# Turning a block's sums by VectorE squares and DRAM in the fourth layer of a graph network

## The chip, the cores and the metric

The kernel runs on one core of a Trainium2 chip. The metric is the device time of one execution in microseconds. A core has five engines that each work through their own instructions in order: TensorE (PE; its weight loads are shown as PEld), VectorE (DVE), ScalarE (ACT), GpSimd (POOL) and SyncE (SP), which here only starts DMAs. They wait for one another through semaphores.

## What is computed

Four layers over 4096 nodes with 256 features each share one adjacency matrix. The change concerns the fourth:

```python
def _cos_normalize(x):
    n = jnp.linalg.norm(x, axis=-1, keepdims=True)
    return x / jnp.maximum(n, COS_EPS)
Qn = _cos_normalize(features @ Wq.T)
Kn = _cos_normalize(features @ Wk.T)
raw_att = Kn @ Qn.T
att = jnp.where(adj > 0, raw_att, NEG) * TEMP
att = jax.nn.softmax(att, axis=1)
prop_fea = att @ features
...
return (1.0 - KEEP_RATIO) * prop_fea + KEEP_RATIO * features
# around it
x = _layernorm(x + _L3_gnn_ref(x, adj, L3_gnn_Wq, L3_gnn_Wk), axis=-1)
```

KEEP_RATIO is 0.5, so a row of the result is 1.5 times the row of x plus half the weighted mean of the features, normalised. The kernel uses that each centred row of x has a known sum, so that the sum of a turned row stands for the softmax's denominator.

## The kernel before

All arrays are float32 on the chip. The fourth layer (cosine_attention, from L1099) takes the 4096 result rows in NB = 8 blocks of 512. For each block it goes over NT = 32 units j of 128 neighbours. A unit's scores are one product of 128x128 by 128x512 (L1115), written to a bank of PSUM: pz holds two (named p), used for even units, ps holds two (named g), used for odd ones after the first block. ScalarE takes the exponential (L1119), VectorE multiplies a pair of units by the mask (L1127) and forms sums and differences of the weights (mix_weights, L434 to L436). TensorE then adds seven products of 128x128 by 128x256 per pair into four accumulating banks, acc 0 to 3 (product, L444), a scheme with seven products in place of eight. A product is two records in the trace.

The text puts the products LAG = 4 units behind the scores: at step i it writes the scores of unit i and then half the products of the pair of unit i - 4. After the last products of a block comes outputs(b). There first_half (L449 to L453) and second_half (L457, L458) combine the four accumulators into c, the "quarters": the features lie on the 128 partitions, the block's 512 rows along the free side. The output wants it the other way round. So turned (L1139) transposes c by TensorE, 128x128 at a time, eight times a block, into the g banks, four to a bank. The row sums of a bank give the inverse of the denominator (halves_of_inverse, L1145 to L1147), rest (L1160 to L1164) adds the scaled row to y, which holds 1.5 x (L1247), and takes its statistics, normalise (L184 and the lines of the root before it) scales the rows, and store (L1167) sends 512 rows of y to the output on SP's queue. The buffers y are two. The last block has an ending of its own.

The order on each engine in this layer is not written by hand, but for the ending. A planner sets it when the program is built: it follows the text's order where it can, and takes an instruction from further on in the text where it expects an engine to be free and the operands to be there. In the three layers before, the order of TensorE, VectorE and ScalarE is the text's.

The masks come by GpSimd's queue (L1046), 512 KB for four units, into four buffers. SP's queue has nothing but the output stores once the first block of this layer is past its first part.

The kernel already turns other data by VectorE and DRAM: turning_apart (L127 to L135) transposes squares of 32x32, stores them with one DMA, and fetches them with four.

Of the kernel before, what the change touches and what calls it, by code (L numbers as in the profile page):

```python
# [9 lines left out]
FP = mybir.dt.float32  # L10
# [4 lines left out]
OP = mybir.AluOpType  # L15
AX = mybir.AxisListType
PSUM = bass.MemoryType.PSUM

P = 128
D = 256  # L20
KC = D // P
QB = 4
QW = QB * P
# [5 lines left out]
def kernel(  # L29
# [27 lines left out]
    nc = tc.nc  # L57
# [4 lines left out]
    def pool(stack, name, bufs, **kw):  # L62
        return stack.enter_context(tc.tile_pool(name=name, bufs=bufs, reuse_waits="tile", **kw))
# [3 lines left out]
    fin = ctx.enter_context(tc.tile_pool(name="fin", bufs=2))  # L67
    fin1 = ctx.enter_context(tc.tile_pool(name="fin1", bufs=1))
# [83 lines left out]
    def one_row(mv, k, y):  # L152
        st = fin.tile([P, 6], FP, name="bn")
        nc.vector.bn_stats(st, y)
        nc.vector.bn_aggr(mv[:, k, :], st)
# [7 lines left out]
    def end_root(v, r, n, eng=nc.vector):  # L163

        s = fin.tile([P, n], FP, name=f"s{n}")
        eng.tensor_tensor(s, r, r, OP.mult)
        eng.tensor_tensor(s, s, v, OP.mult)
        eng.tensor_scalar(s, s, -0.5, 1.5, OP.mult, OP.add)
        eng.tensor_tensor(r, r, s, OP.mult)
# [7 lines left out]
    def begin_root(mv):  # L177
        n = mv.shape[1]
        v = fin.tile([P, n], FP, name=f"v{n}")
        nc.vector.tensor_scalar_add(v, mv[:, :, 1], EPS)  # L180
        return v, first_root(v, n), n

    def scale_row(y, mv, r, k):
        nc.vector.tensor_scalar(y, y, mv[:, k, 0:1], r[:, k:k + 1], OP.subtract, OP.mult)  # L184

    def lift_mean(mv, v, r, eng=nc.vector):

        eng.tensor_tensor(v, v, r, OP.mult)
        eng.tensor_tensor(mv[:, :, 0], mv[:, :, 0], v, OP.subtract)

    def normalise(ys, mv, lift=False):
        v, r, n = begin_root(mv)
        end_root(v, r, n)
        if lift:
            lift_mean(mv, v, r)
        for k, y in enumerate(ys):
            scale_row(y, mv, r, k)
# [249 lines left out]
    def first_half(c, one, acc):  # L447

        nc.scalar.copy(one, acc[3][:, :HW])  # L449
        nc.vector.tensor_tensor(c[:, :2, :], one.unsqueeze(1).to_broadcast([P, 2, HW]),  # L450
                                acc[0].rearrange("p (h i) -> p h i", h=2), OP.add)
        nc.vector.tensor_tensor(c[:, 2, :], c[:, 1, :], acc[1][:, :HW], OP.add)
        nc.vector.tensor_tensor(c[:, 3, :], c[:, 2, :], acc[1][:, HW:], OP.add)  # L453

    def second_half(c, acc):

        nc.vector.tensor_tensor(c[:, 1:3, :], c[:, 1:3, :], acc[2][:, :HW].unsqueeze(1).to_broadcast([P, 2, HW]), OP.add)  # L457
        nc.vector.tensor_tensor(c[:, 1, :], c[:, 1, :], acc[2][:, HW:], OP.add)  # L458

    def quarters(c, k):  # L460

        lo = k % 2 * P
        return [c[:, q, lo:lo + P] for q in ((0, 3), (1, 2))[k // 2]]
# [623 lines left out]
    def cosine_attention(co, tail):  # L1087
# [4 lines left out]
        with ExitStack() as lay:  # L1092
# [1 line left out]
            sb = pool(lay, "co_sb", LAST + 1)  # L1094
            yp = pool(lay, "co_y", 2)
            cp = pool(lay, "co_parts", 1)
            co.turning = (pool(lay, "co_turn", 1), None,
                          pool(lay, "co_turn_far", 2, space=bass.MemoryType.DRAM))

            pa = pool(lay, "co_pa", 1, space=PSUM)  # L1100
            pz = pool(lay, "co_pz", 2, space=PSUM)
            ps = pool(lay, "co_ps", 2, space=PSUM)
            ov = out.rearrange("(t p) d -> p t d", p=P)
            mixed, acc, prob, mix, y = {}, {}, {}, {}, {}
            twice = cp.tile([P, 1], FP, name="twice")
            nc.gpsimd.memset(twice, 2.0 / D)

            def bank():
                return ps.tile([P, QW], FP, name="g")

            def scores(b, j):
                if (b, j // MJ) not in co.mask:
                    co.load_mask(b, j // MJ)
                p = bank() if b and j % 2 else pz.tile([P, QW], FP, name="p")
                nc.tensor.matmul(p.rearrange("p (k i) -> p k i", k=QB), T[j // QB][:, 0, j % QB], T[b][:, 1],  # L1115
                                 start=True, stop=True)
                if j % 2 == 0:
                    prob[b, j // 2] = sb.tile([P, 2, QW], FP, name="prob")
                nc.scalar.activation(prob[b, j // 2][:, j % 2, :], p, AF.Exp)  # L1119
# [11 lines left out]
            def one_product(b, g, n):  # L1131
                product(acc[b], prob[b, g], mix[b, g], mixed[g // 2][:, g % 2], g, n)

            def turned(c, h):

                po = bank().rearrange("p (k f) -> p k f", f=D)
                for k in range(2):
                    for n, quarter in enumerate(quarters(c, 2 * h + k)):
                        nc.tensor.transpose(po[:, k, n * P:(n + 1) * P], quarter, ident)  # L1139
                return po  # L1140

            def halves_of_inverse(po):

                rden = fin.tile([P, 2], FP, name="rden2")
                nc.vector.tensor_reduce(rden, po, AX.X, OP.add)  # L1145
                nc.vector.tensor_scalar_mul(rden, rden, 2.0 / D)
                nc.vector.reciprocal(rden, rden)  # L1147
                return rden

            def sums_turned(b, c, h):  # L1150

                sums = acc[b][3][:, HW + 2 * h:HW + 2 * h + 2]
                for k in range(2):
                    for n, quarter in enumerate(quarters(c, 2 * h + k)):
                        nc.tensor.matmul(sums[:, k:k + 1], quarter, twice, start=(h == k == n == 0), stop=(n == 1),  # L1155
                                         skip_group_check=True)
                return sums

            def rest(b, k, po, rden, mv):
                nc.vector.scalar_tensor_tensor(y[b][:, k, :], po[:, k % 2, :], rden[:, k % 2:k % 2 + 1], y[b][:, k, :],  # L1160
                                               OP.mult, OP.add)
                st = fin.tile([P, 6], FP, name="bn")
                nc.vector.bn_stats(st, y[b][:, k, :])  # L1163
                nc.vector.bn_aggr(mv, st)  # L1164

            def store(b, k, n, eng):
                eng.dma_start(ov[:, b * QB + k:b * QB + k + n, :], y[b][:, k:k + n, :])  # L1167

            def outputs(b):
                c = cp.tile([P, 4, HW], FP, name="quarters")  # L1170
                first_half(c, cp.tile([P, HW], FP, name="one"), acc[b])
                second_half(c, acc[b])
                mv = fin.tile([P, QB, 2], FP, name="mv")
                for h in range(2):
                    po = turned(c, h)
                    rden = halves_of_inverse(po)
                    for k in (2 * h, 2 * h + 1):
                        rest(b, k, po, rden, mv[:, k, :])
                normalise([y[b][:, k, :] for k in range(QB)], mv)
                store(b, 0, QB, nc.sync)  # L1180

            def ending(b):

# [46 lines left out]
            for i in range(len(units) + LAG):  # L1230
                if i < len(units):
                    b, j = units[i]
                    scores(b, j)
                    if j % 2:
                        weights(b, j // 2)
                    if (b, j) == (0, 3):
                        tail(bank, cp)
                    if (b, j) in steps:
                        n, step = steps[b, j]
                        co.prepare(bank, n, step, X[:, n * QB:(n + 1) * QB, :])  # L1240
                if i >= LAG:
                    b, j = units[i - LAG]
                    if j == 0:
                        acc[b] = [pa.tile([P, QW], FP, name=f"acc{n}") for n in range(4)]
                    if j == NT - 8:
                        y[b] = yp.tile([P, QB, D], FP, name="y")
                        nc.scalar.mul(y[b], X[:, b * QB:(b + 1) * QB, :D], 1.5)  # L1247
                    if i - LAG < len(units) - 2 * LAST:
                        for n in range(7)[:4] if j % 2 == 0 else range(7)[4:]:
                            one_product(b, j // 2, n)  # L1250
                        if j == NT - 1:
                            outputs(b)
            with tc.manual_schedule(engines={mybir.EngineType.DVE, mybir.EngineType.Activation}):
                ending(NB - 1)

# [25 lines left out]
    with ExitStack() as weights1, ExitStack() as den1, ExitStack() as weights3:  # L1281
# [26 lines left out]
        co = Cosine(weights3)  # L1308
# [36 lines left out]
```

## Time and profile before

| | |
|---|---|
| runs | 2817.45, 2818.91, 2821.47 us; median 2818.91 |
| the profiled execution | 2817.77 us, of which the span from the first to the last instruction is 2816.0 us |
| granted clock of TensorE | 0.997 |
| the fourth layer's blocks | borders about 76.84 us apart, 2270.5 to 2731.6 us; the end at 2816 |
| TensorE's transposes L1139 | 64 in all, 273 ns each as the records show them |
| VectorE's transposes of 128x512, L127 | about 0.70 us each |
| mask loads of the layer, L1046 | one each 9.5 us, 5.7 us to landing |

The time in the table is that of whole executions. The profile is of one execution. Its page gives for each engine the busy time and its share of the span; a matmul's busy time reaches into that of the next one, so the distance from start to start is its price where TensorE doesn't idle. In lists by time, "x3" is three such instructions merged, and brackets hold the idle time before and what ended it.

### The profile page before, as it was taken

The page shows a single profiled execution, that of the slowest core. Times are in us where ns is not written, and L with a number is a line of the kernel's source. Part 1 is how long each engine was busy: PE and PEld are TensorE (multiplying, and loading weights), DVE is VectorE, ACT ScalarE, POOL GpSimd, SP SyncE. Part 2 cuts the span into 40 slices and gives each one's busy share as a digit, 9 for nine tenths or more (in the row PEclk, how much of TensorE's full clock was granted, in tenths as well). Part 3 has the DMA queues.
Part 4 walks back from the last instruction along what each step waited for, and adds up shares of the span by engine and source line. Part 5 has one row for each costly group of instructions (what it writes and reads, how often), then busy time and mean ns, then how long its engine had stood idle before and what let it go on. Part 6 is the DMA issues. An engine that isn't in the chain of part 4 may idle for free. (4 is left out here: it accounts for less than half of the span.)

```text
span 2816.0 us, 50179 instructions
## 1 busy us (share of the span) xinstructions
PE 2784.7 (99%) x19505; PEld 1434.6 (51%) x19505; DVE 2274.4 (81%) x3034; ACT 1695.6 (60%) x2641; POOL 1050.6 (37%) x983
## 2 busy tenths in 40 slices
PE   9999999999999999999999999999999999999998
PEld 5333333333443333333333334788887777777776
DVE  8899999999677788887887888888877766666665
ACT  8899999999246666666666665555565422222222
POOL 0001001001039878879778782454455100000000
PEclk9999999999999999999999999999999999999999
DMA  7566766665439899898998997576767544444441
GB/s 208 109 136 137 141 144 139 132 136 105 90 96 191 186 184 194 189 194 179 193 186 186 193 184 182 169 201 179 201 186 235 94 67 60 61 67 61 60 58 32
DMA packets 243650, 404.59 MB, mean 144 GB/s; under 512 B 25185, under 2 KB 126033, under 8 KB 242514
## 3 DMA queue, kind: packets, MB, share of 16 engines
q0 software_dynamic: 104176, 182.74, 41.0%
q1 hardware_dynamic: 132720, 211.41, 25.2%
q10 hardware_dynamic: 6514, 7.23, 0.7%
q8 instruction: 153, 2.51, 0.4%
q14 instruction: 87, 0.71, 0.1%
HBM read 332.27 MB, written 35.73 MB: 131 GB/s over the span
## 5 line engine op out<-in xcount | busy, mean ns | idle before, releaser
L830 DVE TENSOR_TENSOR prob<-p,mask 128x1024 f32<-128x1024 f32 x512 | 619.8, 1221 | 168.2 <-ACT p L820 162.1
L820 ACT ACTIVATE p<-p,shift 128x1024 f32<-128x1024 f32 x512 | 555.6, 1088 | 317.8 <-PE p L818 317.8
L310 PE MATMUL acc<-prob,V 128*32 128x512 f32 x6144 | 664.0, 592 | 1.2 <-DVE prob L300 1.2
L297 ACT ACTIVATE prob<-row,dst 128x512 f32<-128x512 f32 x1020 | 635.1, 712 | 0.6
L300 DVE SCALAR_TENSOR_TENSOR prob<-prob,mask 128x2048 f32<-128x2048 f32 x256 | 580.1, 2284 | 25.9 <-ACT prob L297 25.2
L840 POOL TENSOR_TENSOR den<-den,prob 128x1024 f32<-128x1024 f32 x220 | 558.1, 2537 | 95.8 <-DVE prob L830 84.9
L818 PE MATMUL p<-qT,kT 64*64 64x512 f32 x4096 | 531.1, 590 | 0.8 <-DVE prob L830 0.8
L854 PE MATMUL acc<-prob,V 64*64 64x512 f32 x4096 | 529.9, 589 | 0.0
L310 PEld LDWEIGHTS acc<-prob,V 128*32 128x32 f32 x6144 | 197.3, 110 | 453.0 <-issue 431.6
L444 PE MATMUL acc<-mix,mixed 128*128 128x256 f32 x1440 | 390.0, 380 | 1.7 <-DVE quarters L458 1.0
L854 PEld LDWEIGHTS acc<-prob,V 64*64 64x64 f32 x4096 | 157.4, 133 | 282.1 <-issue 280.3
L818 PEld LDWEIGHTS p<-qT,kT 64*64 64x64 f32 x4096 | 154.4, 133 | 277.4 <-issue 257.4
L444 PEld LDWEIGHTS acc<-mix,mixed 128*128 128x128 f32 x1440 | 272.2, 190 | 42.1 <-PE acc L444 2.9
L1127 DVE TENSOR_TENSOR prob<-prob,mask 128x1024 f32<-128x1024 f32 x128 | 156.4, 1222 | 168.9 <-ACT prob L1119 167.0
L90 POOL COPY tick<-prob 128x1 f32<-128x1 f32 x35 | 38.5, 1100 | 642.4 <-DVE prob L300 641.5
L444 PE MATMUL acc<-prob,X 128*128 128x256 f32 x960 | 250.5, 380 | 8.6 <-DVE quarters L450 8.6
L846 POOL DMA_DIRECT2D den<-prob x240 | 226.8, 945 | 59.0 <-DVE prob L830 26.0
L1046 POOL DMA_DIRECT2D mask<-in_adjT x64 | 47.7, 745 | 516.7 <-DVE prob L1127 430.3
L565 DVE SCALAR_TENSOR_TENSOR prob<-r,own,mask 128x512 f32<-128x512 f32 x252 | 177.1, 743 | 64.0 <-POOL mix L436 21.3
L444 PEld LDWEIGHTS acc<-prob,X 128*128 128x128 f32 x960 | 181.6, 190 | 92.2 <-issue 62.4
L1119 ACT ACTIVATE prob<-p 128x512 f32<-128x512 f32 x144 | 86.1, 598 | 222.1 <-PE p L1115 209.8
L1119 ACT ACTIVATE prob<-g 128x512 f32<-128x512 f32 x112 | 66.8, 596 | 194.0 <-PE g L1115 194.0
(220 smaller groups left out, 2810.3 us busy)
## 6 DMA issues: line engine op xcount, KB each, us to landing
mask<-in_adjT SPq DMA_DIRECT2D x254, 512.0 KB
den<-prob POOLq DMA_DIRECT2D x240, 512.0 KB, 5.2
mask<-edges SPq DMA_DIRECT2D x512, 64.0 KB
mask<-in_adjT POOLq DMA_DIRECT2D x64, 512.0 KB, 5.7
edges<-in_adj POOLq DMA_DIRECT2D x32, 512.0 KB, 10.0
far<-squares SPq DMA_DIRECT2D x16, 512.0 KB
den<-prob SPq DMA_DIRECT2D x16, 512.0 KB
row<-far SPq DMA_DIRECT2D x7, 1024.0 KB
```

Source lines behind the costliest of these rows:

```text
L297: nc.scalar.activation(z[:, h, :], r, AF.Relu, bias=-1.0, scale=dst[:, j, h:h + 1])
L300: nc.vector.scalar_tensor_tensor(z, z, 1.0, mask[m][:, j % MJ, :].unsqueeze(1).to_broadcast([P, H, QW]), OP.add, OP.mult)
L310: nc.tensor.matmul(acc[b][h * G:(h + 1) * G, n, :], part, prob[b, j][:, h, :], start=(j == 0), stop=(j == NT - 1))
L444: nc.tensor.matmul(acc[at][:, half * HW:(half + 1) * HW], w, a, start=(g == 0 and half == 0), stop=(g == NP - 1), skip_group_check=True)
L565: nc.vector.scalar_tensor_tensor(z[:, n, :], r, ga.own[:, j:j + 1], mask[:, n, :], OP.add, OP.mult)
L818: nc.tensor.matmul(p[c * d:(c + 1) * d, r, :], kT[half, c, at:at + d], qT[half, c, cols], start=True, stop=True)
L820: nc.scalar.activation(p, p, AF.Exp, bias=shift)
L830: nc.vector.tensor_tensor(z, p, mask[m][:, j % MJ, :].unsqueeze(1).to_broadcast([P, KC, QW]), OP.mult)
L840: nc.gpsimd.tensor_tensor(to, to, flat, OP.add)
L846: nc.gpsimd.dma_start(to, flat, accum_op=OP.add)
L854: nc.tensor.matmul(acc[b][c][r * d:(r + 1) * d, :], V[half, j, r * d:(r + 1) * d], prob[b, j][half, r, :], start=(j == 0), stop=(j == NH - 1))
L1127: nc.vector.tensor_tensor(z, z, co.mask[b, 2 * g // MJ][:, lo:lo + 2, :], OP.mult)
```

## The change

For all blocks but the last the sums are no longer transposed by TensorE. outputs(b) now makes c and calls squares_far for each half. That turns two quarters of 128x256 by VectorE in squares of 32x32 into sq, starts four stores on SP's queue, each of 32 partitions and in pieces of 32 numbers (128 B), to the DRAM tile away, and one load of 128 rows of 2 KB from it to the tile t. What was done with the turned sums is in outputs_far(b), which the text calls in the next block after the products of unit 10: the sums of t's rows, the inverse, the addition to y, the statistics, the normalisation and the store. The tiles sq, and t of the second half, lie in buffers of the pool fin1 that earlier layers use; t of the first half is new.

```diff
             def outputs(b):
                 c = cp.tile([P, 4, HW], FP, name="quarters")
                 first_half(c, cp.tile([P, HW], FP, name="one"), acc[b])
+                squares_far(b, 0, (c[:, 0, :], c[:, 3, :]))
                 second_half(c, acc[b])
-                mv = fin.tile([P, QB, 2], FP, name="mv")
-                for h in range(2):
-                    po = turned(c, h)
-                    rden = halves_of_inverse(po)
-                    for k in (2 * h, 2 * h + 1):
-                        rest(b, k, po, rden, mv[:, k, :])
-                normalise([y[b][:, k, :] for k in range(QB)], mv)
-                store(b, 0, QB, nc.sync)
+                squares_far(b, 1, (c[:, 1, :], c[:, 2, :]))
...
+            def squares_far(b, h, both):
+
+                B = P // QB
+                sq = fin1.tile([P, QW], FP, name=f"kept{h}").rearrange("p (a k c s) -> p a k c s", a=QB, k=2, c=KC)
+                for n, quarter in enumerate(both):
+                    nc.vector.transpose(sq[:, :, :, n, :].rearrange("p a k s -> p k a s"),
+                                        quarter.rearrange("p (k a r) -> p k a r", k=2, r=B))
+                away = far.tile([B, QB, QW // P, QB, B], FP, name="away")
+                for q in range(QB):
+                    nc.sync.dma_start(away[:, :, :, q, :].rearrange("r a m s -> r (a m) s"),
+                                      sq[q * B:(q + 1) * B].rearrange("r a k c s -> r (a k c) s"))
+                t = (fin1 if h else cp).tile([P, QW], FP, name="kept2")
+                nc.sync.dma_start(t, away.rearrange("r a m q s -> a r (m q s)"))
+                back[b, h] = t.rearrange("p (k f) -> p k f", k=2)
+
+            def outputs_far(b):
+                mv = fin.tile([P, QB, 2], FP, name="mv")
+                rden = fin.tile([P, QB], FP, name="rden4")
+                for h in range(2):
+                    nc.vector.tensor_reduce(rden[:, 2 * h:2 * h + 2], back[b, h], AX.X, OP.add)
+                nc.vector.tensor_scalar_mul(rden, rden, 2.0 / D)
+                nc.vector.reciprocal(rden, rden)
+                for k in range(QB):
+                    nc.vector.scalar_tensor_tensor(y[b][:, k, :], back[b, k // 2][:, k % 2, :], rden[:, k:k + 1], y[b][:, k, :],
+                                                   OP.mult, OP.add)
+                    one_row(mv, k, y[b][:, k, :])
+                normalise([y[b][:, k, :] for k in range(QB)], mv)
+                store(b, 0, QB, nc.sync)
...
                         if j == NT - 1:
                             outputs(b)
+                    if b and j == 10:
+                        outputs_far(b - 1)
```

More of the change, by code (lines that the diff above doesn't have):

```diff
@@ L1096, in cosine_attention @@
             cp = pool(lay, "co_parts", 1)
-            co.turning = (pool(lay, "co_turn", 1), None,
-                          pool(lay, "co_turn_far", 2, space=bass.MemoryType.DRAM))
+            far = pool(lay, "co_turn_far", 2, space=bass.MemoryType.DRAM)
+            co.turning = pool(lay, "co_turn", 1), None, far
             pa = pool(lay, "co_pa", 1, space=PSUM)
@@ L1103, in cosine_attention @@
             ov = out.rearrange("(t p) d -> p t d", p=P)
-            mixed, acc, prob, mix, y = {}, {}, {}, {}, {}
+            mixed, acc, prob, mix, y, back = {}, {}, {}, {}, {}, {}
             twice = cp.tile([P, 1], FP, name="twice")
@@ L1140, in turned @@
                 return po
[L1142 to L1148, printed above, removed]
             def sums_turned(b, c, h):
```

## The prediction

> **What bounds the kernel now.** I read the page's first two parts, then the busy time by stretches of the fourth layer, then TensorE's instructions in order of time across one border between blocks, then the waits.
>
> ```profile
> PE 2784.7 (99%) x19505; PEld 1434.6 (51%) x19505; DVE 2274.4 (81%) x3034; ACT 1695.6 (60%) x2641; POOL 1050.6 (37%) x983
> ```
>
> A busy TensorE need not be the limit by this line alone. The stretches say that in this layer it is. Columns: stretch, its length, then the busy time of PE, PEld, DVE, ACT and POOL, the granted clock, the DMA share and GB/s.
>
> ```profile
> 2347.35:2424.19 76.84, 76.84 (x297) 55.36 (x297) 52.04 (x97) 20.74 (x36) 5.92 (x9) 1.00 0.42 62
> 2424.19:2501.03 76.84, 76.84 (x297) 55.35 (x297) 52.04 (x97) 20.73 (x36) 5.92 (x9) 1.00 0.42 62
> ```
>
> A block takes 76.84 us and TensorE idles for none of it; VectorE has 24.8 us to spare, DMA over half. So what TensorE no longer does is won, and what makes it wait is lost. How much is transposes? TensorE by time, across one border:
>
> ```profile
> 2418.41 1.03 PE L444 MATMUL acc<-prob,X 128*128 128x256 f32 x4
> ...
> 2422.29 0.27 PE L1139 MATMUL g<-ident,quarters 128*128 128x128 f32 x1
> 2422.40 1.02 PE L1115 MATMUL p<-T,T 128*128 128x512 f32 x2
> 2423.26 0.59 PE L444 MATMUL acc<-prob,X 128*128 128x256 f32 x2
> 2423.70 0.49 PE L1139 MATMUL g<-ident,quarters 128*128 128x128 f32 x3
> 2424.02 0.60 PE L444 MATMUL acc<-prob,X 128*128 128x256 f32 x2
> ...
> 2425.75 0.60 PE L1139 MATMUL g<-ident,quarters 128*128 128x128 f32 x4
> 2426.19 0.60 PE L444 MATMUL acc<-mix,mixed 128*128 128x256 f32 x2
> ```
>
> Busy times of matmuls overlap; the price is start to next start: 0.11 + 0.32 + 0.44 = 0.87 us for the eight of a block. Undisturbed, a pair of units repeats every 4.738 us (the chain of waits has pieces at 2390.15 and 2418.58, six periods apart), so a block's 16 pairs are 75.81 us, and 76.84 - 75.81 = 1.03 us is all that a border costs. The 0.16 us beyond the transposes lies just after: the score matmul of the odd unit needs a g bank, both hold turned sums, and it comes late and out of its order (at 2428.42, behind the even one at 2427.05).
>
> [...] Here a 256 KB store of squares and the load behind it lie 3.7 to 6.7 us apart in this layer (SP issues at 2176.58 and 2180.31; 2235.09 and 2241.81). [...] No data packet of 128 B is in the trace. [...]
>
> **The change, part by part.**
>
> *Removed:* for seven of eight blocks the eight transposes and both g banks' occupation: 7 x 1.03 = 7.2 us of TensorE, with nothing beneath it.
>
> *VectorE.* Four transposes of 128x256 a block. The 128x512 ones took 0.70 us, so I take 0.38 each, 1.5 us (ends 0.35 and 0.5). Reduction, inverse, addition, statistics and scaling stay, reading SBUF instead of PSUM; no gain taken. 52.0 + 1.5 of 76.8 us is hidden in 24.8 us of slack. One place is tighter: first_half's two turns come before second_half, whose last add (L458, ended 2425.4) frees acc 2. With the g banks free the order returns to score, four products, score, three products, and acc 2's first product falls at about 2422.29 + 3 x 0.87 (score, four products as two pairs) + 0.87 (score) + 0.43 (one product), about 2426.2. One turn fits in the 0.96 us that VectorE idles before L452, the other moves L458 to 2425.8. Nothing is lost; without that gap L458 ends at 2426.2, so 0 to 0.3 us a block is at stake. I take 0.02.
>
> *SP.* Ten issues a block (eight stores, two loads) at some 0.43 us: 4.3 us. SP does nothing else there but the output store; its wait on a load holds only the next half's transfers and that store. The store comes later, and the ACT instruction that waits for it (L1247) already sits 1.8 to 2.5 us idle on it in every block; y has two buffers, so nothing else waits.
>
> *DMA engines.* A half is 4 stores of 512 packets of 128 B. Hardware queue packets of 4 B took 8.9 ns (500 in 1731 to 1733 us: 13.9% of 16 engines x 2 us), those of about 1 KB took 45 ns (2640 in 2300 to 2740 us at 1.7%). In between, 13.5 ns: 2048 x 13.5 / 16 = 1.7 us a half. Both halves and the loads add some 6% of DMA time to 42%. Masks are four buffers deep, a load each 9.5 us, so they don't come late. Bounds: 1.1 us at the 4 B price; above, the one store of many small packets in the trace, far<-src, 512 packets of 4 B, after which SP waited about 10 us each time.
>
> *The new wait.* outputs_far's first reduction needs the load. VectorE runs in order, so behind it stand the mask multiplications (L1127) and weight sums that TensorE needs. When does it stand at the head? Not necessarily where the text has it: the order in this layer is the planner's, and it moves ready work forward, as with y's scaling (L1247), written eight units before a block's end and run at 2287.49 for the block of 2347 to 2424, over 110 us ahead, as soon as its DMA was expected. So the reduction will be put at the expected landing, and the wait is what the chip takes longer than expected. The trace has two kinds of such wait, for work that the planner drew forward behind a DMA (first from 2270 to 2740 us, then from 2170 to 2270):
>
> ```profile
> ACT y L1247 <- DMA out<-y: 11.9, 6, 2.5
> ```
> ```profile
> DVE squares L127 <- DMA far<-squares: 3.3, 2, 2.5
> ```
>
> The columns are total, times, longest. One landing surprises by 0.8 to 2.5 us. The new chain has two, a store and a load: 1.6 to 5.0 us, I take 3.3. What can TensorE bear? The steady rhythm:
>
> ```profile
> 2410.66 1.02 PE L1115 MATMUL g<-T,T 128*128 128x512 f32 x2
> ...
> 2417.55 1.02 PE L1115 MATMUL p<-T,T 128*128 128x512 f32 x2
> 2418.41 1.03 PE L444 MATMUL acc<-prob,X 128*128 128x256 f32 x4
> ```
> ```profile
> 2412.35 1.23 DVE L1127 TENSOR_TENSOR prob<-prob,mask 128x1024 f32<-128x1024 f32 x1 [1.87 <-ACT prob L1119]
> 2413.61 0.69 DVE L434 TENSOR_TENSOR mix<-prob 128x512 f32<-128x512 f32 x1
> 2414.34 0.42 DVE L435 TENSOR_TENSOR mix<-prob,mix 128x256 f32<-128x256 f32 x1
> ```
>
> The pair scored at 2410.66 is masked by 2413.58 and first used at 2418.41, 4.8 us later; the sum ready at 2414.76 is used by the third product at 2419.27, 4.5 us later. So VectorE may stand 4.5 us, up to 5.7 where the wait begins at the head of its 1.87 us gap (1.87 less 0.69 for the reduction). 3.3 us is below that and costs nothing. Without this cover it would cost 7 x 3.3 = 23 us.
>
> Sum: -7.2 + 7 x 0.02 = -7.1 us against the profiled execution, 2817.77 us (span 2816.0 and 1.8 around it), so 2810.7. The median of the runs is 1.1 us higher, so **2812**.
>
> **Rivals.**
>
> *A, the wait outgrows the cover (slower).* Place: the first reduction of outputs_far, seven times. Price: the wait less 4.5 us, less the 1.03 gained; it decides from a wait of 5.5 us. For it: 128 B pieces, [...] SP's queue holding the second half's chain behind the first, and far<-src. If the stores suffer once what far<-src did beyond an ordinary store (10 against 3.7 us, so 6.3 more), the wait is 9.6 us, each block loses 9.6 - 5.5 = 4.1, and the time is 2819 + 29 = 2848. If all four stores suffer in turn, 40 us a half, it is hundreds of microseconds. Against: the pieces of far<-src are 4 B inside one 2 KB row, these are 32 times as long over 256 KB; and from 2429 to 2435 us the DMA is nearly idle.
>
> *B, the gain is mostly eaten (no change).* A wait of 4.7 to 6.3 us, or acc 2 freed 0.5 to 1 us late at each border, gives 2815 to 2822; I price it at 0.7 us a block: 2817. For it: both margins are estimates within a microsecond of their limits.
>
> *C, no drawing forward.* The reductions stay at their written place, unit 10, some 24 us after the border, long after the landing; the burst there is like the one at 2425.64 to 2430.5 in the kernel before, which stopped TensorE for 0.16 us at most. 7 x 0.87 us gained: 2818.9 - 6.1 = 2813. Only the trace tells it from the forecast. Against it: the early run of L1247 and of the mixed features.
>
> **How the numbers follow.** Forecast 0.44, A 0.34, B 0.13, C 0.09. A measurement of this kernel tells about 0.2%, 5.6 us, from no change. The gain of 7.1 us is barely over it, so about a tenth of the forecast's chance falls into no change, and half of C's; B is mostly no change, with a little on either side; A is slower. Faster 0.46, same 0.18, slower 0.36. The forecast's own range, from the 0 to 0.3 us at acc 2 and the spread of the runs, is 2809 to 2815. For 8 in 10 it reaches through B into A, up to 2842; beyond that are the heavy cases of A, about 0.17.
>
> **What would show it.** Right: in the seven blocks L1139 is gone and block periods are 75.8 to 75.9 us with TensorE still busy throughout; the odd score is no longer behind the even one; VectorE's wait for the load is under 4.5 us, well before unit 10. Wrong: a TensorE idle on prob or mix a few microseconds after the reduction's wait (A); a TensorE idle on quarters L457 or L458 at the border (B); the reductions some 24 us after the border with no wait (C). The forecast falls if the period is above 76.1 us.

## The result, and the profile after

The changed kernel takes 2813.65 us (median of 22 runs, 2811.65 to 2816.82); the kernel before, run beside it, 2819.72. The ratio is 0.9981, 95% interval 0.9976 to 0.9987: 5.4 us faster (3.7 to 6.8). One of the 22 executions of the kernel before took 10528 us, the others 2816 to 2822; the comparison leaves it out. The profiled execution took 2813.03 us, its span 2811.2.

TensorE's line on the page of the kernel after:

```profile
PE 2776.7 (99%) x19449; PEld 1427.4 (51%) x19449; DVE 2285.6 (81%) x3048; ACT 1694.8 (60%) x2641; POOL 1049.9 (37%) x983
```

56 matmuls are gone, 7 x 8, and the share is still 99%: again this line says nothing about where the limit is. The stretches of two blocks of the fourth layer after, cut at ScalarE's copy L449, with which each block's output begins (columns as in the prediction):

```profile
2342.04:2417.95 75.91, 75.91 (x290) 54.64 (x289) 53.50 (x99) 20.73 (x38) 5.94 (x8) 1.00 0.48 76
...
2493.86:2570.61 76.75, 76.44 (x290) 54.47 (x289) 53.30 (x99) 20.29 (x37) 5.94 (x8) 1.00 0.48 76
```

76.84 us have become 75.91, with TensorE busy throughout, in five of the six blocks from border to border, and the last block is as much shorter. The block after the fourth border takes 76.75, and there TensorE idles for 0.31 us. VectorE (53.5 us) and the DMA (0.48) stand where the prediction put them. Now TensorE in order of time across the first border after:

```profile
2269.31 1.02 PE L1115 MATMUL p<-T 128*128 128x512 f32 x2
2270.17 1.03 PE L444 MATMUL acc<-prob,X 128*128 128x256 f32 x4
2271.03 1.03 PE L444 MATMUL acc<-mix,mixed 128*128 128x256 f32 x4
2271.89 1.02 PE L1115 MATMUL g<-T 128*128 128x512 f32 x2
2272.75 0.59 PE L444 MATMUL acc<-mix,X 128*128 128x256 f32 x2
2273.21 0.67 PE L444 MATMUL acc<-mix,mixed 128*128 128x256 f32 x2
2273.71 0.59 PE L444 MATMUL acc<-prob,mixed 128*128 128x256 f32 x2
```

No transpose is left, and the g score stands in its place between p scores. The steady distance of two halves of a product is 0.43 us; here the starts 2272.75, 2273.21 and 2273.71 are 0.46 and 0.50 apart. The late product is acc 2's first. These 0.10 us are all that an ordinary border still costs beyond 75.81.

The waits of the kernel after, 2260 to 2740 us (total, times, longest):

```profile
ACT y L1262 <- DMA out<-y: 18.2, 6, 5.4
DVE rden L1170 <- DMA kept<-away: 6.4, 6, 4.3
```

The new wait on VectorE adds up to 6.4 us there (7.2 to the end of the layer), about 1.0 a block, but 4.3 of it come at once. ScalarE's wait for the output store, longest 2.5 us before, has become 5.4. The long wait on VectorE, at the fourth border:

```profile
2516.89 0.69 DVE L434 TENSOR_TENSOR mix<-prob 128x512 f32<-128x512 f32 x1
2521.91 0.69 DVE L1170 TENSOR_REDUCE rden<-kept 128x2 f32<-128x512 f32 x1 [4.33 <-DMA kept<-away]
2522.52 0.42 DVE L435 TENSOR_TENSOR mix<-prob,mix 128x256 f32<-128x256 f32 x1
```

and TensorE beside it:

```profile
2521.69 1.03 PE L444 MATMUL acc<-prob,X 128*128 128x256 f32 x4
2522.99 1.13 PE L444 MATMUL acc<-mix,mixed 128*128 128x256 f32 x4 [0.27 <-DVE mix L435]
```

The planner put the second reduction between L434 and L435 of a pair. The weight sum behind it came late, and TensorE with it: rival A, once, for 0.84 us (76.75 - 75.91). Half of that, 0.44 us, is the late start at 2522.99 (due at 2522.55, four records of 0.216 us after 2521.69); the rest lies in the starts just after it.

**Where the 5 us are.** At the last border's L449 the two profiles stand at 2793.98 and 2789.01 us. Seven times 0.93 us is -6.51, the late landing +0.84, and +0.69 was there before the first border, which the layers before reach at 2265.4 to 2268.3 us from one execution to another, experiments that leave VectorE's order to the planner included. The sum, -4.98, is the 4.97 seen. The blocks alone, -5.67, lie inside the interval of the whole executions.

### The profile page after: what moved, and what is told of

Same layout as the page of the kernel before. It is cut to its first block, busy times and chain, and to the rows that moved or that the text cites. A ratio compares the mean times of both kernels' runs of the same rounds, so it can differ in the third digit from the quotient of the medians.

```text
span 2811.2 us, 50179 instructions
## 1 busy us (share of the span) xinstructions
PE 2776.7 (99%) x19449; PEld 1427.4 (51%) x19449; DVE 2285.6 (81%) x3048; ACT 1694.8 (60%) x2641; POOL 1049.9 (37%) x983
## 3 DMA queue, kind: packets, MB, share of 16 engines
q8 instruction: 152, 2.49, 0.4%
```

## The experiments

Theory: TensorE's own time is won, and the planner lays the reductions where it expects the landing; what is left over is acc 2's late release and one landing that surprises. Rivals: the DMA chain itself costs time beside the visible wait; half of the gain is not the transposes but something else in the output; the reductions cost nothing only because of where the text has them.

**The floor and one half.** The first kernel leaves the transposition out altogether, the second turns the first half as before on TensorE and only the second through DRAM.

```diff
-                squares_far(b, 0, (c[:, 0, :], c[:, 3, :]))
...
-                squares_far(b, 1, (c[:, 1, :], c[:, 2, :]))
+                back[b, 0] = back[b, 1] = c.rearrange("p q i -> p (q i)")[:, :QW].rearrange("p (k f) -> p k f", k=2)
```

> Leaves out the turning altogether for the seven blocks: no transposes on any engine, no stores and loads of the sums; VectorE's work on the output rows stays and reads the unturned quarters. Theory (the change wins TensorE's time and all it adds is hidden): block periods of 75.81 us where the changed kernel has 75.91, no stall, and a time within 2 us of the changed kernel's, at 2812 to 2813. Rival (the stores, the load and the wait cost several microseconds that are hidden in a larger gain): 2808 or less, or periods clearly below 75.8.

```diff
-                squares_far(b, 0, (c[:, 0, :], c[:, 3, :]))
+                h0 = turned(c, 0)
                 second_half(c, acc[b])
+                kept = cp.tile([P, QW], FP, name="kept2")
+                nc.scalar.copy(kept, h0.rearrange("p k f -> p (k f)"))
+                back[b, 0] = kept.rearrange("p (k f) -> p k f", k=2)
```

> Turns the first half of each block by TensorE as before (ScalarE copies it out of its bank), the second half by VectorE and DRAM. Theory (the transposes' own 0.11 us each is the gain, and a single held bank costs nothing): a period of 75.81 + 0.44 = 76.25, with what is left at acc 2 up to 76.35; about 3.5 us above the changed kernel. Rival (the held banks, not the transposes, are what counts): 76.7 or more, or below 76.0.

A block's stretch, first without the transposition:

```profile
2417.80:2493.61 75.81, 75.81 (x290) 54.72 (x289) 51.91 (x95) 20.72 (x37) 5.92 (x8) 1.00 0.42 63
```

and with half of it on TensorE:

```profile
2344.09:2420.35 76.26, 76.26 (x294) 55.05 (x293) 52.64 (x97) 21.13 (x39) 5.93 (x8) 1.00 0.45 69
```

Measured: 2811.36 us, ratio 0.997 (0.9959 to 0.9982), and 2814.57, ratio 0.9982 (0.9974 to 0.999). The first is a little under the 2812 to 2813 that the theory expected. Without any turning a block takes 75.81 us, the six from border to border alike: the pair rhythm read from the kernel before, with nothing added at the border. So the change leaves 7 x 0.10 + 0.84 = 1.5 us of this floor untaken. With four transposes on TensorE a block takes 0.44 us more, half of the 0.87 us of all eight: most of the gain is the transposes' own time, and one g bank held, which ScalarE empties here, costs nothing. The time is 0.9 us above the changed kernel's, not the 3.5 expected: by the blocks 7 x 0.34 = 2.4 us are lost, but the 0.84 us at the fourth border are not.

**Larger pieces, and the second half's sums first.** In the third kernel the DRAM tile is ordered so that the stores are pieces of 512 B and the load runs over 128 rows of it; the reductions and additions then read the rows in another order, by more and smaller instructions of VectorE. The fourth adds one more move: second_half before the first half's squares.

```diff
-                away = far.tile([B, QB, QW // P, QB, B], FP, name="away")
+                away = far.tile([QB, B, QB, P], FP, name="away")
...
-                    nc.sync.dma_start(away[:, :, :, q, :].rearrange("r a m s -> r (a m) s"),
-                                      sq[q * B:(q + 1) * B].rearrange("r a k c s -> r (a k c) s"))
+                    nc.sync.dma_start(away[:, :, q, :].rearrange("a r m -> r a m"),
+                                      sq[q * B:(q + 1) * B].rearrange("r a k c s -> r a (k c s)"))
...
-                nc.sync.dma_start(t, away.rearrange("r a m q s -> a r (m q s)"))
+                nc.sync.dma_start(t, away.rearrange("a r q m -> (a r) (q m)"))
...
```

> The same way through DRAM, but with each row of t in another order, so that a store moves pieces of 512 B in place of 128 B and the load reads 128 rows from one contiguous area. Theory (small pieces cost little here, 12.6 ns each[...]): the store lands at most 2 us sooner, the load sooner too, VectorE's wait of 7.2 us in all goes to about zero, the period stays 75.91, the time within 2 us of the changed kernel. Rival A (small pieces hold the transfers up): landings several microseconds sooner and all blocks at 75.9 with a time 3 us lower or more.

```diff
-                squares_far(b, 0, (c[:, 0, :], c[:, 3, :]))
                 second_half(c, acc[b])
+                squares_far(b, 0, (c[:, 0, :], c[:, 3, :]))
                 squares_far(b, 1, (c[:, 1, :], c[:, 2, :]))
```

> As the one with 512 B pieces, and the first half's two turns are written after the adds that free acc 2 instead of before. Theory (0.10 us a border is acc 2 freed late): period 75.81, TensorE's late product at the border gone, some 0.7 us less than with the turns before. Rival (the 0.10 us is something else): 75.91 stays.

SP at the second border, with pieces of 128 B (the kernel after):

```profile
2347.43 5.41 SPq L1160 DMA_DIRECT2D away<-kept  x6
2353.92 0.56 SPq L1163 DMA_DIRECT2D kept<-away  x1
2354.53 1.24 SPq L1160 DMA_DIRECT2D away<-kept  x2
2359.99 0.56 SPq L1163 DMA_DIRECT2D kept<-away  x1
```

and with pieces of 512 B:

```profile
2347.42 3.55 SPq L1160 DMA_DIRECT2D away<-kept  x7
2353.27 0.34 SPq L1163 DMA_DIRECT2D kept<-away  x1
2353.65 0.43 SPq L1160 DMA_DIRECT2D away<-kept  x1
2356.34 0.34 SPq L1163 DMA_DIRECT2D kept<-away  x1
```

Seven stores are issued in 3.55 us where six took 5.41, and the second load starts 3.7 us sooner. Yet the waits of the third kernel on VectorE grew:

```profile
DVE rden L1170 <- DMA kept<-away: 19.4, 13, 3.6
```

The reductions had moved forward too, to 13.1 to 14.6 and 16.6 to 19.9 us after the border's first add (17.4 to 17.9 and 22.8 to 27.3 in the kernel after). Both the theory's "no wait" and the rival's gain missed: a faster transfer doesn't shorten a wait where the planner also puts the waiting instruction sooner. In time: 2814.61 us, ratio 0.9981 (0.9974 to 0.9989), the same as the change; blocks of 75.91 and one of 76.24. The thirteen waits cost nothing but 0.33 us at the fourth border, where 1.89 and 3.17 us fell close together.

The fourth kernel's stretches:

```profile
2344.12:2419.93 75.81, 75.81 (x290) 54.72 (x289) 54.16 (x105) 20.61 (x37) 5.93 (x8) 1.00 0.47 76
2419.93:2495.75 75.82, 75.82 (x290) 54.73 (x289) 54.16 (x105) 20.41 (x38) 5.92 (x8) 1.00 0.47 77
```

This is the floor, and the other blocks agree to 0.01 us. The 0.10 us came with the first half's turns in front of L458. Its time, 2812.97 us, ratio 0.9977 (0.9968 to 0.9986), isn't distinguishable from the change's by whole executions; by the blocks of the two profiled executions it is 1.5 us better.

**The turns' order alone,** with the pieces of 128 B left as they are, and the place in the text moved from unit 10 to unit 24:

```diff
+                second_half(c, acc[b])
                 squares_far(b, 0, (c[:, 0, :], c[:, 3, :]))
-                second_half(c, acc[b])
```

> The changed kernel with its 128 B pieces, the first half's turns written after the adds that free acc 2. Theory: period 75.81 in place of 75.91, first store some 2 us later, one block may still stall on a late landing. Rival: 75.91 stays.

```diff
-                    if b and j == 10:
+                    if b and j == 24:
```

> Only the place in the text of the output work changes: after unit 24 of the next block in place of unit 10. Theory (the planner draws it forward to the landing that it expects, so the written place doesn't count): first reduction 17 us after the border's first add, second 24 us, period 75.91, no change of time. Rival C (the written place sets it): the reductions some 57 us after the border, no wait for the load at all.

The first gave five blocks of 75.81 or 75.82 us from border to border and one of 76.55 (2813.74 us in one run): the acc 2 term goes with the order of the turns and the late landing doesn't. With the place moved by 14 units the reductions stayed at 17.4 and, but for the fourth border, 22.8 to 23.4 us after the first add (2814.17 us in one run), blocks at 75.91, the one after the fourth border 77.34 with a wait of 4.93 us. So under the planner the written place doesn't count, between these two.

**VectorE's order by hand.** What does it cost if nothing is drawn forward? In two kernels VectorE keeps the text's order in the layer, with outputs_far at unit 10 and at unit 4.

```diff
+            with tc.manual_schedule(engines={mybir.EngineType.DVE}):
                 for i in range(len(units) + LAG):
...
-                    if b and j == 10:
+                        if b and j == 4:
```

> VectorE's order in this layer is the text's (by hand), the output work in one piece after unit 10. Theory: at some 26 us after the border the load has landed, so no wait for it; but the output work is one burst of about 8 us, longer than the cover of 4.5 to 5.7 us, so TensorE loses 2 to 4 us a block: 2828 to 2842. Rival (a burst of 8 us is hidden): 2814.

> As the one before, but the output work after unit 4: VectorE gets to the first reduction some 12 us after the border, the second half lands some 24 us after it. Theory (a wait beyond the cover costs TensorE its full length): 10 to 12 us of waiting in each block on top of the burst, so 70 to 85 us above the kernel with unit 10. Rival (TensorE has more cover than worked out, or the load lands much sooner when nothing else delays it): less than 35 us above.

Unit 10: 2823.49 us, ratio 1.0016 (1.0009 to 1.0023), and blocks of 76.93 us. No landing is waited for; the burst of output work in one piece, 8.9 us (2375.78 to 2384.71 us), makes TensorE idle for 0.21 us just behind it, at 2385.89, waiting for a masked pair. A block costs 76.93 - 75.81 = 1.12 us over the floor, less than the 2 to 4 expected and more than the 0.16 that rival C allowed. By the distances of TensorE's starts 0.8 us of it lie behind the burst; most of the rest lies at the border, where VectorE's first add now stands 5.5 us after L449 and not 0.8. A block is then no shorter than in the kernel before (76.84), so the change doesn't pay when the whole order of VectorE is the text's. How much of this is the burst's being in one piece, and how much the rest of that order, was not taken apart: 4 of the 10 us above the changed kernel stand before the first border (2270.21 us against 2266.12), where there is no output work yet.

Unit 4: 2840.54 us, ratio 1.0075 (1.0058 to 1.0091). VectorE waits at both reductions of every border, from 2260 to 2790 us:

```profile
DVE rden L1170 <- DMA kept<-away: 54.7, 14, 8.1
```

Expected were 70 to 85 us above the kernel with unit 10, measured 17. One reason is that the waits are shorter, 7.8 us a block and not 10 to 12. The other is that they don't cost their full length, although the burst behind them already uses up the cover in the kernel with unit 10. TensorE's waits for masked pairs in the same stretch:

```profile
PE acc L444 <- DVE prob L1127: 15.8, 7, 5.4
```

At the second border VectorE gives TensorE nothing from 2362.1 us, the end of a weight sum, to 2380.0, the end of the next masked pair, and TensorE idles for only 2.1 of these 17.9 us. Its order was still the planner's, which can reckon with a VectorE held up by its own order, and ten scores stand in a row here at every border; at unit 10, where VectorE is away for 10 us, it is three. The ten at the first border, from 2291.76 to 2300.35 us, whose products follow later:

```profile
2291.76 1.02 PE L1115 MATMUL p<-T,T 128*128 128x512 f32 x2
...
2299.49 1.02 PE L1115 MATMUL g<-T,T 128*128 128x512 f32 x2
2301.44 0.91 PE L444 MATMUL acc<-prob,X 128*128 128x256 f32 x3 [0.93 <-DVE prob L1127]
```

So 54.7 us of waits left 24.4 us in the blocks (their excess over 75.81 from 0.73 to 8.41), and 16.5 when the 7.9 of unit 10 are taken off, which fits the 17 between the two times. Some 4 of them went by at half the clock (see the last section). A wait that the order provides for costs about a third here; that the planner put the scores there because it foresaw the wait is argued from their number, not shown.

**Why the fourth border?** SP there, in the kernel after:

```profile
2499.25 5.37 SPq L1160 DMA_DIRECT2D away<-kept  x6
2507.01 0.56 SPq L1163 DMA_DIRECT2D kept<-away  x1
2507.61 1.24 SPq L1160 DMA_DIRECT2D away<-kept  x2
2516.59 0.55 SPq L1163 DMA_DIRECT2D kept<-away  x1
```

The second half's last two stores stand behind the first load's wait, and from them to the second load pass 9.0 us, against 5.5 at the second border. In the DMA queues' packets from 2503 to 2505.5 us (count, MB, share) one thing is out of the ordinary, the last line:

```profile
q1 hardware_dynamic: 2805, 0.35, 89.4%
q0 software_dynamic: 82, 0.07, 17.0%
q8 instruction: 1, 0.02, 2.4%
```

The page lists q8 as a queue of kind instruction; its 152 packets in this execution carry 2.49 MB, 16 KB each. By that name they are taken here as fetches of instructions; the page names no engine for them, and that they are TensorE's, as the expectation below has it, is the author's reading. In four kernels (the change, the late turns, unit 24 and the one shifted by 8 below) such a fetch on q8 begins 0.3 to 1.3 us after the fourth border's first store packet; at their borders that are in time it begins 1.9 us or more after it, or is not there. To move the fetches against the borders, two kernels have 8 and 16 more matmuls in front of the first layer.

```diff
-                warm(2)
+                warm(10)
```

> The changed kernel with 8 more warming matmuls at the very start, whose results nothing reads: they move TensorE's 16 KB instruction fetches of the fourth layer some 4 us to the front, measured from each border. Theory (the fourth border lands late because such a fetch falls into its stores, 1.2 us after their first packet): now no fetch falls there, at no border, so no border lands late and all periods are 75.91. Rival (the fourth border is late for another reason): 76.7 stays at the fourth border.

```diff
-                warm(2)
+                warm(18)
```

> The same with 16 more: fetches some 8 us to the front, so that the one that came 9.2 us after the third border's first store packet comes about 1 us after it. Theory: the late landing moves from the fourth border to the third. Rival: it stays at the fourth.

With 8 (2814.51 us in one run) the expectation failed: at the fourth border a fetch still fell 0.8 us after the first store packet, and it was still late there. The fetches nearest to the borders had not moved evenly: by 6.6 us at the third border, 4.0 at the seventh, 0.4 at the fourth. With 16 (2812.73 us in one run) the lateness left the fourth border and turned up at the third (fetch at 1.1 us) and at the seventh (0.7 us). At the third, the second load was issued 8.6 us after the last stores, as late as at the fourth in the change. VectorE's reductions that then waited:

```profile
2444.80 0.69 DVE L1170 TENSOR_REDUCE rden<-kept 128x2 f32<-128x512 f32 x1 [3.49 <-DMA kept<-away]
...
2749.36 0.69 DVE L1170 TENSOR_REDUCE rden<-kept 128x2 f32<-128x512 f32 x1 [4.39 <-DMA kept<-away]
```

All six late borders in these five kernels go with such a fetch, and adding matmuls moved the lateness, to one place that was foreseen and one that was not. The other traces agree: the two kernels with VectorE's order by hand have a fetch 1.8 and 1.1 us after the first store packet at their fourth border, and the latest second load there.

How the delay grows to several microseconds can be followed further. The change's mask load (the masks are bfloat16 on the chip, not float32) is issued 13.8 us after L449. At all eight late borders (the second load issued 21.6 us or more behind L449, elsewhere at most 20.8) the last store was issued after the mask load (by 0.03 to 0.8 us), at all the other borders of the seven kernels with pieces of 128 B for both halves before it. The pieces of 512 B, whose last store always precedes the mask load, also meet a fetch at the fourth border (1.0 us in the third kernel, 0.5 in the fourth); there the second load is only 0.3 to 1.6 us later than elsewhere. So about a microsecond of the delay goes with the fetch alone, and the rest with falling behind the mask load. Both go together in every case here, which is no proof of how the queues do it: no run moves the mask load alone.

**What a surprise costs.** These runs give the loss of the block against the length of the wait that fell into it:

| kernel, border | wait of the second reduction, us | loss of the block, us |
|---|---|---|
| shifted by 16, third | 3.49 | 0 |
| late turns, fourth | 4.11 | 0.74 |
| the change, fourth | 4.33 | 0.84 |
| shifted by 16, seventh | 4.39 | 0.90 |
| unit 24, fourth | 4.93 | 1.43 |
| shifted by 8, fourth | 3.67 | 1.08 |

At 3.49 us nothing is lost; from 4.33 to 4.93 the loss grows by 0.59 us for 0.60 us of wait. In these four rows the reduction stands between L434 and L435, and in the three with a loss TensorE's first late start comes later by the wait less 3.9 us (0.44, 0.49 and 1.03 us). In the kernel with the late turns the reduction stands behind L436, and its loss appears one pair later. The last row doesn't fit, and has mostly another cause: 0.2 us lie just behind the reduction, 0.9 us here. ScalarE, and then TensorE, in that kernel:

```profile
2539.70 1.06 ACT L1262 ACTIVATE y<-X 128x1024 f32<-128x1024 f32 x1 [6.29 <-DMA out<-y]
```
```profile
2542.55 0.70 PE L444 MATMUL acc<-prob,X 128*128 128x256 f32 x2 [0.30 <-DVE prob L1127]
```

The late reduction made the output store late. ScalarE's scaling of a later block's y, drawn forward as well, waited for the store, and behind it stood the exponentials. In the kernel after the same wait is 5.4 us at its longest, and TensorE doesn't idle behind it.

## Why the prediction was right

The mechanism and the sign were right. That the wait cost almost nothing is in part luck: the cover was smaller than forecast, but so was the wait. Of the forecast's steps:

- **Removed, 1.03 us a block.** Right. The floor's 75.81 us is the predicted rhythm, and half of the transposes gives half of their time.
- **acc 2, taken as 0.02 of a possible 0 to 0.3.** Mis-sized: 0.10 us, in every block, taken away by the order of the turns alone. One turn did fit into the idle time before L452, as forecast, and the other took 0.36 us from start to start. But the planner also put L436, 0.33 us, ahead of L458:

```profile
2424.14 0.41 DVE L436 TENSOR_TENSOR mix<-prob,mix 128x256 f32<-128x256 f32 x1
2424.47 0.41 DVE L458 TENSOR_TENSOR quarters<-quarters,acc 128x256 f32<-128x256 f32 x1
```

So L458 ended 6.9 us after the border's L449, not 6.7 as forecast (6.3 in the kernel before). That is still 0.12 us before the product's turn, and it came late all the same; the forecast had taken any end before that turn as free.
- **The new wait, taken as 3.3 us a block.** About 1.0, from 0 to 4.3. That the planner would draw the reductions forward was right, and unit 24 shows that the place in the text is no bound. But the reductions stand 17 and 23 us after the border's first add: both the planner's place and the chip's chain lie further out than the forecast thought, and only their difference is waited for. The second is not "well before unit 10", which the forecast puts at some 24 us; only the run with unit 24 tells it from rival C.
- **The cover, taken as 4.5 to 5.7 us.** Taken too wide. Where the reduction stands between L434 and L435, without the 1.87 us gap in front of it, its own 0.69 us also comes off: 4.5 - 0.69 = 3.8 us. This fits the 3.9 us measured at three late borders. With this cover the assumed wait of 3.3 us was half a microsecond from costing time in every block: the forecast had less room than it said.
- **A surprise in one block.** Left out of the sum, as the wait was one value for all blocks; it cost 0.84 us once.
- **"y has two buffers, so nothing else waits".** Wrong as a rule: L1262 waited up to 6.29 us with the exponentials behind it, and cost 0.9 us once. In the change it cost nothing.
- **DMA and SP.** 0.48 of DMA time, as predicted; 12.6 ns for a packet of 128 B (2406 packets at 95.0% of 16 engines, 2276 to 2278 us), against 13.5. The 128 packets of 2 KB of one load took 3.3 us, 3.7 of them in flight on average by their own times (2355.26 to 2358.57 us); with the load over 128 rows, in the third kernel, 1.5 us and 10 (2354.26 to 2355.71 us). A store's issue took 0.63 us in the median, not 0.43, all of it hidden in the ordinary blocks. The store of squares that the forecast calls 256 KB is one of 512 KB (the new ones are 64 KB each).
- **Rivals.** A's mechanism exists and came into force once instead of seven times; for that surprise its price was too low, as the cover is 3.9 us at L435 and not 4.5, and the starts behind a late one lose 0.4 us more; for waits that the order provides for (unit 4) it doesn't hold. B's figure was not reached. C fell: the reductions don't stay at their written place, and with VectorE in the text's order a block costs 1.12 us over the floor, not 0.16 at most, so that its gain of 0.87 us a block would have been gone.

In the profiles the sum was -7.1 us against 4.97 measured at the last border: 0.56 less for acc 2, 0.84 for the late landing, 0.69 for the start of the layer, which differs by up to 3 us between these executions and is no part of the change.

## What to carry to other kernels

When a planner orders an engine that waits for a DMA, ask by how much the landing can differ from what the planner expects, not how long the transfer takes: with the larger pieces a faster transfer was only planned closer, and at unit 4 a wait that the order provided for was partly filled with other work. Work out the cover at the place where the waiting instruction will stand, take off that instruction's own time, and look at the worst of the landings rather than their mean. When an engine is the limit of a stage, first run the stage without the disputed step: the floor shows what is left to win.

## What the runs showed of the hardware

**Small pieces.** Stores in pieces of 128 and of 512 B give the same kernel time (ratio 0.9981 for both, though VectorE's instructions differ too), and the DMA is busy for less than half of a block with either (0.48 in the kernel after, 0.47 in the fourth kernel). What the smaller ones cost is SP's time, 0.90 us a store in the burst of six against 0.51 in that of seven (the fifth of the small ones alone held SP for 2.1 us), and a second load issued 3.7 us later.

**TensorE's clock after short idles.** In the kernel with unit 4 half the clock was granted after an idle of 2.14 us:

```profile
2380.06 2.08 PE L444 MATMUL acc<-prob,X 128*128 128x256 f32 x4 [2.14 <-DVE prob L1127]
```

A group of four took 2.08 us instead of 1.03, and from start to start a record took 0.43 us instead of 0.22. After an idle of 2.27 us, in front of 2460.35 us, the clock stayed whole. The stretches of both (the clock is the third column from the end):

```profile
2380.00:2382.00 2.00, 1.94 (x5) 1.58 (x6) 1.90 (x5) 0.00 (x0) 0.00 (x0) 0.50 0.75 254
2460.00:2462.00 2.00, 1.65 (x8) 1.44 (x9) 1.90 (x5) 0.00 (x0) 0.00 (x0) 1.00 0.75 262
```

So in this trace the clock was halved after an idle of 2.14 us and whole after a longer one of 2.27 us. By the distances of the starts 1.6 us were lost here, and 2.5 us after an idle of 5.35 us at 2536.82: these are the 4 us of unit 4's loss.
